# Moving the output weights' means within the filling of a two-layer kernel, with second PSUM banks for projections and center taps

## The chip, the cores and the metric

The kernel runs on one core of a Trainium2 chip. Its engines run side by side, each through its own queue in order, and wait for one another by semaphores: TensorE (PE, the matrix products, which write to PSUM), VectorE (DVE), ScalarE (ACT), GpSimd (POOL, which also issues DMAs that add onto their destination) and SyncE (SP, which only issues DMAs). PSUM has eight banks of 128 partitions by 512 fp32 values. The metric is the time of one execution on the device in microseconds; lower is better.

## The reference, cut to what matters

Two layers work on an image batch of 2 x 768 channels x 64 x 64, all in fp32. Only layer 0 is touched by the change. Cut to its core:

```python
x = gn(x) @ in_proj_w.T                      # 768 -> 1536 channels
xs = depthwise_conv3x3(x, conv_w) + conv_b   # nine taps per channel
xs = xs * sigmoid(xs)                        # SiLU
dt, Bs, Cs = split(xs @ x_proj_w.T, [48, 52])
delta = softplus(dt @ dt_w.T + dt_b)
s[l] = exp(delta * A) * s[l-1] + delta * xs * Bs      # scan over 4096 positions, 4 states
y = sum(s * Cs) + D * xs
y = (y - mean(y)) * rsqrt(var(y) + 1e-5) * ln_g + ln_b
out = x_in + y @ out_proj_w.T
```

Layer 1 (group norm, projection, an attention-like weighting per head, output projection) follows.

The normalization of y is folded into the output weights: a row of the weights (one of the 1536 inner channels) is multiplied by `ln_g`, and from each output column its mean over the 1536 channels is subtracted, so that the mean of y drops out of the product. `ln_b` gives a bias of each output channel. The changed weights are written to DRAM once, and read back from there in layer 0.

## The kernel before

Layer 0 is cut into 16 tiles (eight rows of an image, 512 positions) times 12 chunks of 128 inner channels, 192 units in all. The function `step(g)` issues one step of a software pipeline written out by hand: `manual_schedule` keeps the order of the text on every engine, so the order of the calls in `step` is the order of each queue. One step works on different units at once:

- `n = g + 17`: the projection `in_proj(n)` on TensorE, six chunks of 128 input channels into one bank, then `in_proj_evict(n)`, which ScalarE does into one of two padded buffers `xs_bufs[n % 2]`. For the first 12 units `row0(n)` computes the image's first row apart, into the bank "pz" (`psZ`), and ScalarE copies it to `carry`.
- `a = g + 15`: the nine taps of the 3 x 3 convolution. ScalarE writes the center tap into the PSUM tile `acc` (`tap_act`, issued a step ahead for a + 1), TensorE can add taps onto it with a diagonal (`diag`, `taps_pe`), VectorE adds taps with one fused multiply-add each (`taps_dve`), the last of them writing the result u to SBUF. Some taps go another way: ScalarE multiplies them into buffers (`taps_act`), and GpSimd's DMAs add these up and then onto u (`taps_dma_sum`, `taps_dma`). Tables say which taps go where: `FILL_DMA_TAPS` and `FILL_PE_TAPS` for a < 15.
- `silu(a - 4 ..)` for four units at a time, with a table load of ScalarE ahead and one behind, and then `x_proj_pair` on TensorE; every fourth step.
- `g` itself: softplus, exponentials, the scan on VectorE (`scan`, lines 512 and 514), products with C (line 521), sums by GpSimd and its DMAs.
- `g - 12`: the output projection, with weights read from `wo_dr`.

The first 16 calls, `step(-17)` to `step(-2)`, with v = 0 to 15, are the **filling**: only n and a are in range, so there are projections and taps but no scan. In step v the projection is number v and the taps are those of v - 2. During the filling the statistics of the second image are also gathered (`gn_load`, `gn_piece`, one or two pieces a step on VectorE), and the output weights are made ready in this order:

- in the steps v = 2 to 5, SP loads the 12 chunks of the weights into `wg` (line 246);
- at the end of step 7, `out_weights_rows`: 72 matmuls into a bank "po0", and three copies by ScalarE;
- at the end of step 8, `out_weights_mean`: the sums spread over the partitions into `wm` ("po0", "po1") and the bias into `pb` ("st"), and copies by ScalarE;
- after the steps 8 to 15, one or two chunks each: ScalarE's scaling (line 276) and right behind it the subtraction of the means (line 277), by GpSimd for the first chunk and by VectorE for the second; SP stores a chunk to `wo_dr` after the next step (line 280).

The pool that holds `wg` is closed after the filling, and the buffers of the steady part (B and C in `bc`, `das`, `s`, `tm_bufs`) take its place in SBUF, so they can be written only when the stores have read `wg`. From `step(-1)` on come these buffers, and from `step(0)` the scans.

PSUM in the filling: one bank "psa" for projections (odd ones from n = 12 on also use "po0"), one bank "acc" for center taps, two for "pz", one for "px", "po0", "po1" and "st".

Of the kernel before, what the change touches and what calls it, by code (L numbers as in the profile page):

```python
# [7 lines left out]
F32 = mybir.dt.float32  # L8
# [6 lines left out]
P = 128  # L15
# [6 lines left out]
KM = DM // P  # L22
KI = DI // P
# [21 lines left out]

DMA_TAPS = ((0, 2, 6), (0, 2, 6), (0, 2, 6), (0, 2))
PE_TAPS = ((), (), (), (1, 7))
FILL_DMA_TAPS = ((0, 2), (0, 2), (0, 2), ())  # L50
FILL_PE_TAPS = ((), (), (), (1,))

AHEAD = 15
BEHIND = 12
# [13 lines left out]
def both_layers(  # L68
# [192 lines left out]
            nc.scalar.copy(rows[32 * j : 32 * j + 2, :], gb[32 * j : 32 * j + 2, :MG])  # L261

    def out_weights_mean(rows, wmean, pick):
        pb = psS.tile([P, 512], F32, tag="st", name="pbo")
        wm = [psO.tile([P, 512], F32, tag=f"po{e}", name=f"pwm{e}") for e in range(2)]
        for j in range(KM // 2):
            for e in range(2):
                m = 2 * j + e
                nc.tensor.matmul(pb[:, m : m + 1], rows[:, e * P : (e + 1) * P], pick[:, j, P : P + 1], start=True, stop=True)
            nc.tensor.matmul(wm[j // 2][:, j % 2 * MG : (j % 2 + 1) * MG], pick[:, j, :P], rows, start=True, stop=True)  # L270
        nc.scalar.copy(wmean[:, : 2 * MG], wm[0])
        nc.scalar.copy(wmean[:, 2 * MG :], wm[1][:, :MG])
        nc.scalar.copy(bias_o, pb[:, :KM])

    def out_weights_scale(wg, wmean, k, engine):
        nc.scalar.activation(wg[:, k, :], wg[:, k, :], AF.Copy, scale=pc[:, k, PC_G : PC_G + 1])
        engine.tensor_sub(wg[:, k, :], wg[:, k, :], wmean)

    def out_weights_store(wg, k):
# [63 lines left out]
    def in_proj(n):  # L343
        i, c, b, t = where(n)
        nn = TL if t < NT - 1 or b + 1 < NB else TL - W
        w = wis.pop(n)
        if KI <= n < AHEAD + 2 and n % 2:
            pa = psO.tile([P, 512], F32, tag="po0", name=f"pa{n}")
        else:
            pa = psA.tile([P, 512], F32, tag="psa", name=f"pa{n}")  # L350
        for k in range(KM):
            nc.tensor.matmul(pa[:, :nn], w[:, k, :], xts[i, k][:, :nn], start=(k == 0), stop=(k == KM - 1))  # L352
# [20 lines left out]


    def dma_taps(a):
        return (DMA_TAPS if a >= AHEAD else FILL_DMA_TAPS)[a % 4]

    def pe_taps(a):
        return (PE_TAPS if a >= AHEAD else FILL_PE_TAPS)[a % 4]

    def diag(a):
        c = a % KI
# [3 lines left out]
        dgs[a] = dg  # L386

    def tap_act(a):
        acc = psC.tile([P, 512], F32, tag="acc", name=f"acc{a}")
        nc.scalar.activation(  # L390
            acc.rearrange("p (h w) -> p h w", w=W), xs_bufs[a % 2][:, 1 : 1 + TR, 1 : 1 + W], AF.Copy,
            scale=pc[:, a % KI, PC_W + 4 : PC_W + 5],
        )
        accs[a] = acc
# [47 lines left out]
    def silu(a):  # L442
        nc.scalar.activation(us[a], us[a], AF.Silu, bias=pc[:, a % KI, PC_CB : PC_CB + 1])  # L443
# [667 lines left out]
    with tc.manual_schedule():  # L1111
# [31 lines left out]
        def step(g, prep=None):  # L1143
# [46 lines left out]
            if 0 <= a + 1 < NQ0:  # L1190
                diag(a + 1)

            do_silu = g % 4 == 1 and 0 < a <= NQ0
            do_soft = g % 2 == 1 and 0 <= g + 1 < NQ0
            if do_silu:
                nc.scalar.preload_act_table_set(SILU_SET)
                for q in range(4):
                    silu(a - 4 + q)
            if do_soft:
                nc.scalar.preload_act_table_set(SOFTPLUS_SET)  # L1200
                softplus_pair(g + 1)
# [89 lines left out]
                prep()  # L1291
            if do_silu:
                for q in range(0, 4, 2):
                    x_proj_pair(a - 4 + q)
            if v == len(by_step) + 1:
                gn_aggregate(1)
                norms[g + 2] = gn_finish(1)
# [7 lines left out]
        with tc.tile_pool(name="l0st", bufs=1, side="right") as sp:  # L1305
            wg = sp.tile([P, KI, DM], F32, name="wg")
            rows = sp.tile([P, MG], F32, name="gb_rows")
            nc.vector.memset(rows, 0.0)
            wmean = sp.tile([P, DM], F32, name="wmean")
            pick = sp.tile([P, KM // 2, P + 1], F32, name="pick")  # L1310
            nc.sync.dma_start(pick, pick_in)

            first = -AHEAD - 2
            ready_w = {8: (0,), 9: (1, 2), 10: (3,), 11: (4, 5), 12: (6, 7), 13: (8, 9), 14: (10,), 15: (11,)}
            prep = {7: lambda: out_weights_rows(wg, rows), 8: lambda: out_weights_mean(rows, wmean, pick)}
            for v in range(AHEAD + 1):
# [199 lines left out]
```

## Time and profile before

| | us |
|---|---|
| median of 3 runs | 3758.63 (3756.74 to 3765.8) |
| profiled execution | 3758.2 |
| its span | 3756.3 |

The page adds up each engine's busy time over the span, and then by 40 slices. A digit of 9 is 90% or more of a slice. The filling lies in the first 206 us, some two slices.

| in the filling, from the trace | value |
|---|---|
| projection 1 (line 352, twelve records) starts | 61.96 us |
| taps of unit 0 on VectorE (line 436) start | 70.70 us |
| `out_weights_rows` on TensorE | 113.0 to 118.4 us |
| `out_weights_mean` on TensorE | 125.8 to 128.4 us |
| scaling (line 276), ScalarE | 12, median 927 ns, first 128.9, last 198.4 us |
| subtraction (line 277), GpSimd | 8, 1799 to 2117 ns |
| subtraction (line 277), VectorE | 4, 1853 to 2175 ns |
| stores (line 280), SP | 12, first 131.8, last 201.5 us |
| first scan product (line 512) starts | 209.65 us |

Rows of the order of time have the start in us, the duration in us, engine, line, operation, what is written from what, how many were merged, and in brackets the idle time of the engine just before and what ended it. A row with `u<-xs,pc,acc` is the last tap of a unit. TensorE's merged rows end somewhat late, since ends of matmuls are modelled: the distance from one start to the next is the better measure where rows follow one another closely.

### The profile page before, as it was taken

What the parts mean: (1) busy time and instruction counts of PE and PEld (TensorE: products, weight loads), DVE (VectorE), ACT (ScalarE), POOL (GpSimd) and SP (SyncE); (2) the same over time, 40 slices, a digit from 0 to 9 for tenths busy, and PEclk for the clock granted to TensorE, in tenths of its full rate; (3) what the DMA queues carried; (4) which work ended last, traced back from release to release, by engine and by line L of the source; (5) the groups of instructions that cost most, each with busy time, mean ns of one, the idle gap of its engine ahead of it and who ended that gap; (6) DMA issues with size and microseconds to landing.
All of it is one profiled execution on the core that took longest, in us unless ns stands there. A gap on an engine that the chain in (4) does not pass through costs nothing.

```text
span 3756.3 us, 36987 instructions
## 1 busy us (share of the span) xinstructions
PE 3558.0 (95%) x10882; PEld 1719.9 (46%) x10882; DVE 2842.8 (76%) x2554; ACT 2562.5 (68%) x4940; POOL 1742.7 (46%) x1761
## 2 busy tenths in 40 slices
PE   5877999999999999999999999999999999999999
PEld 3422433333333333333343343333344458886688
DVE  7699999999999999999999999997710162224522
ACT  2588888889888888889788888897633441244221
POOL 0245565555555556555555655654413214320232
PEclk9988999999999999999999999999999999999999
DMA  9677898989989899898898989996656428764487
GB/s 352 182 176 149 187 207 177 209 196 202 203 183 202 190 212 202 186 205 182 200 205 189 211 176 207 201 197 170 150 144 191 141 75 271 253 214 125 150 270 243
DMA packets 371081, 730.80 MB, mean 195 GB/s; under 512 B 43280, under 2 KB 105168, under 8 KB 366784
## 3 DMA queue, kind: packets, MB, share of 16 engines
q0 software_dynamic: 145632, 269.03, 42.1%
q1 hardware_dynamic: 225248, 459.41, 37.2%
q8 instruction: 88, 1.44, 0.2%
q14 instruction: 113, 0.93, 0.1%
HBM read 433.88 MB, written 60.03 MB: 131 GB/s over the span
## 4 chain that ended last, share of the span: by engine, by line
PE 39%; DVE 37%; ACT 10%; DMA 6%; issue 6%; POOL 2%; SPq 0%; DVEq 0%; POOLq 0%; ACTq 0%
DVE s L514 14%; DVE acc L436 8%; PE po_p L852 6%; PE po L574 6%; DVE da L521 6%; DVE s L512 5%; PE pa L352 5%; PE psa_p L852 4%; PE acc_p L852 4%; PE mmp L663 4%; DMA u<-ysum 3%; PE pq L663 3%; PE mmp L694 2%; ACT tm L402 1%; ACT da L489 1%
## 5 line engine op out<-in xcount | busy, mean ns | idle before, releaser
L352 PE MATMUL pa<-u,w 128*128 128x512 f32 (+1 forms) x2304 | 1046.8, 605 | 20.2 <-ACT carry L367 13.6
L574 PE MATMUL po<-u,w 128*128 128x512 f32 x2304 | 1035.9, 599 | 18.5 <-DVE u L586 18.5
L514 DVE TENSOR_TENSOR_SCAN s<-da,s 128x2052 f32<-128x2052 f32 x192 | 851.1, 4433 | 19.5 <-ACT u L307 0.5
L352 PEld LDWEIGHTS pa<-u,w 128*128 128x128 f32 x2304 | 433.8, 193 | 619.4 <-issue 489.6
L574 PEld LDWEIGHTS po<-u,w 128*128 128x128 f32 x2304 | 428.9, 190 | 610.8 <-issue 557.8
L501 POOL TENSOR_TENSOR ysum<-da 128x1024 f32<-128x1024 f32 x192 | 385.0, 2005 | 576.9 <-DVE da L521 467.8
L436 DVE SCALAR_TENSOR_TENSOR acc<-xs,pc,acc 128x512 f32<-128x512 f32 x741 | 558.1, 753 | 39.4 <-PE acc L422 13.0
L489 ACT ACTIVATE da<-dl,neg_a 128x512 f32<-128x512 f32 x768 | 489.7, 713 | 0.0
L512 DVE TENSOR_TENSOR s<-du,bc 128x2048 f32<-128x2048 f32 x192 | 438.8, 2285 | 55.1 <-POOL du L493 54.8
L408 POOL DMA_DIRECT2D tm<-tm x309 | 268.0, 867 | 447.1 <-ACT tm L402 385.1
L521 DVE TENSOR_TENSOR da<-s,bc 128x2048 f32<-128x2048 f32 x192 | 440.0, 2292 | 6.3
L508 POOL DMA_DIRECT2D u<-ysum x384 | 378.8, 1250 | 3.7 <-issue 2.6
L390 ACT ACTIVATE acc<-xs,pc 128x512 f32<-128x512 f32 x192 | 132.3, 689 | 282.5 <-DVE u L436 281.2
L402 ACT ACTIVATE tm<-xs,pc 128x512 f32<-128x512 f32 x486 | 317.1, 717 | 4.8 <-DMA tm<-tm 3.3
L493 POOL TENSOR_TENSOR du<-dl,u 128x512 f32<-128x512 f32 x192 | 244.2, 1272 | 0.0
L414 POOL DMA_DIRECT2D u<-tm x177 | 205.2, 1159 | 56.5 <-issue 29.8
L852 PE MATMUL po_p<-u,w 128*128 128x256 f32 x630 | 159.2, 382 | 0.0
L436 DVE SCALAR_TENSOR_TENSOR u<-xs,pc,acc 128x512 f32<-128x512 f32 x192 | 143.6, 748 | 9.5 <-DVE acc L436 0.4
L477 PE MATMUL pz<-xd,dt_w 48*128 48x512 f32 x384 | 113.6, 670 | 37.0 <-DVE gs_x L193 13.9
L663 PE MATMUL pq<-u,w 128*128 128x512 f32 x312 | 140.4, 596 | 1.9 <-ACT u L651 1.8
L505 ACT ACTIVATE u<-u,pc 128x512 f32<-128x512 f32 x192 | 137.0, 714 | 2.1 <-POOL du L493 2.1
L443 ACT ACTIVATE u<-u,pc 128x512 f32<-128x512 f32 x192 | 124.4, 712 | 15.0 <-DMA u<-tm 14.4
(286 smaller groups left out, 4749.0 us busy)
## 6 DMA issues: line engine op xcount, KB each, us to landing
u<-ysum POOLq DMA_DIRECT2D x384, 256.0 KB, 5.7
tm<-tm POOLq DMA_DIRECT2D x309, 256.0 KB, 4.4
w<-in_wP SPq DMA_DIRECT2D x192, 384.0 KB, 5.1
w<-wo_dr SPq DMA_DIRECT2D x192, 384.0 KB, 4.9
u<-x SPq DMA_DIRECT2D x274, 256.0 KB, 5.4
w<-s_dr_p SPq DMA_DIRECT2D x240, 192.0 KB, 3.7
u<-tm POOLq DMA_DIRECT2D x177, 256.0 KB, 5.8
bc<-bc_dr SPq DMA_DIRECT2D x32, 1024.0 KB, 7.1
```

Of the source, the lines that this page charges most:

```text
L352: nc.tensor.matmul(pa[:, :nn], w[:, k, :], xts[i, k][:, :nn], start=(k == 0), stop=(k == KM - 1))
L402: nc.scalar.activation(tm.rearrange("p (h w) -> p h w", w=W), xs[:, dy : dy + TR, dx : dx + W], AF.Copy, scale=pc[:, c, PC_W + j : PC_W + ...
L436: nc.vector.scalar_tensor_tensor(dst, xs[:, dy : dy + TR, dx : dx + W], pc[:, c, PC_W + j : PC_W + j + 1], acc, ALU.mult, ALU.add)
L489: nc.scalar.activation(das[g % 2][:, n, 1:], deltas[g], AF.Exp, scale=neg_a[:, c, n : n + 1])
L501: nc.gpsimd.tensor_add(ysum[:, 0 : 2 + g % 2 : 1 + g % 2, :], da[:, 0:2, 1:], da[:, 2:4, 1:])
L508: nc.gpsimd.dma_start(us[g], ysums(g, n), accum_op=ALU.add)
L512: nc.vector.tensor_mul(s[:, :, 1:], dus.pop(g).unsqueeze(1).to_broadcast([P, NS, TL]), bc[:, :NS, :])
L514: nc.vector.tensor_tensor_scan(sf, das[g % 2].rearrange("p n l -> p (n l)"), sf, 0.0, ALU.mult, ALU.add)
L521: nc.vector.tensor_mul(das[g % 2][:, :, 1:], s[:, :, 1:], bc[:, NS:, :])
L574: nc.tensor.matmul(po[e], w[:, kk, e * P : (e + 1) * P], us[i * KI + k], start=(k == 0), stop=(k == KI - 1))
L663: nc.tensor.matmul(pa, w[:, k, :], x1s[b, j, k], start=(k == 0), stop=(k == KM - 1))
L852: nc.tensor.matmul(dst, half[:, k, :], tiles[blocks[seq[i][0]][:3]][what][k], start=(start and k == 0), stop=(k == KH - 1), skip_group_che ...
```

## The change

All of it is in the filling.

- The center tap's tile alternates between the banks "st" (even a) and "acc" (odd a) for a < 15. The bias `pb`, which used "st", now lies in the second half of the tile `wm`, and `wm` itself in the two banks of "pz".
- Projections with odd n below 17 use "po1", from n = 1 on; even ones "psa".
- All units of the filling but 11 have the DMA taps 0 and 2 and no PE tap; unit 11 has the PE tap 1 and no DMA taps. Before, this was so for 3, 7 and 11.
- SiLU and `x_proj_pair` of units 0 to 3 move from step 6 to step 8, those of 4 to 7 from step 10 to step 12. Those of 8 to 11 stay in step 14.
- `out_weights_rows` and `out_weights_mean` both move to the end of step 11.
- Chunks are scaled three after each of the steps 11 to 14. Two of three (all three after step 14) are subtracted by GpSimd right behind; the third by VectorE after the following step. All three are stored after the following step.

```diff
-FILL_DMA_TAPS = ((0, 2), (0, 2), (0, 2), ())
-FILL_PE_TAPS = ((), (), (), (1,))
+FILL_DMA_TAPS = (0, 2)
+FILL_PE_TAPS = (1,)
...
     def out_weights_mean(rows, wmean, pick):
-        pb = psS.tile([P, 512], F32, tag="st", name="pbo")
-        wm = [psO.tile([P, 512], F32, tag=f"po{e}", name=f"pwm{e}") for e in range(2)]
+        wm = psZ.tile([P, 2, 512], F32, tag="pz", name="pwm")
+        pb = wm[:, 1, MG : MG + KM]
...
-    def out_weights_scale(wg, wmean, k, engine):
+    def out_weights_scale(wg, k):
         nc.scalar.activation(wg[:, k, :], wg[:, k, :], AF.Copy, scale=pc[:, k, PC_G : PC_G + 1])
+
+    def out_weights_sub(wg, wmean, k, engine):
         engine.tensor_sub(wg[:, k, :], wg[:, k, :], wmean)
...
-        if KI <= n < AHEAD + 2 and n % 2:
-            pa = psO.tile([P, 512], F32, tag="po0", name=f"pa{n}")
+        if n < AHEAD + 2 and n % 2:
+            pa = psO.tile([P, 512], F32, tag="po1", name=f"pa{n}")
...
     def dma_taps(a):
-        return (DMA_TAPS if a >= AHEAD else FILL_DMA_TAPS)[a % 4]
+        return DMA_TAPS[a % 4] if a >= AHEAD else FILL_DMA_TAPS if a != KI - 1 else ()
     def pe_taps(a):
-        return (PE_TAPS if a >= AHEAD else FILL_PE_TAPS)[a % 4]
+        return PE_TAPS[a % 4] if a >= AHEAD else FILL_PE_TAPS if a == KI - 1 else ()
+    def silu_of(a):
+        if a < KI:
+            return {6: 0, 10: 4}.get(a)
+        return a - 4 if a % 4 == 0 and a <= NQ0 else None
...
     def tap_act(a):
-        acc = psC.tile([P, 512], F32, tag="acc", name=f"acc{a}")
+        bank, tag = (psS, "st") if a < AHEAD and a % 2 == 0 else (psC, "acc")
+        acc = bank.tile([P, 512], F32, tag=tag, name=f"acc{a}")
...
-            do_silu = g % 4 == 1 and 0 < a <= NQ0
+            first4 = silu_of(a)
+            do_silu = first4 is not None
...
-                    silu(a - 4 + q)
+                    silu(first4 + q)
...
-                    x_proj_pair(a - 4 + q)
+                    x_proj_pair(first4 + q)
...
-            ready_w = {8: (0,), 9: (1, 2), 10: (3,), 11: (4, 5), 12: (6, 7), 13: (8, 9), 14: (10,), 15: (11,)}
-            prep = {7: lambda: out_weights_rows(wg, rows), 8: lambda: out_weights_mean(rows, wmean, pick)}
+            scaled_w = {11: ((0, 1), (2,)), 12: ((3, 4), (5,)), 13: ((6, 7), (8,)), 14: ((9, 10, 11), ())}
+            def means():
+                out_weights_rows(wg, rows)
+                out_weights_mean(rows, wmean, pick)
             for v in range(AHEAD + 1):
                 if 2 <= v < 6:
                     out_weights_load(wg, 3 * (v - 2))
-                step(first + v, prep.get(v))
+                step(first + v, means if v == 11 else None)
...
-                for k, engine in zip(ready_w.get(v, ()), (nc.gpsimd, nc.vector)):
-                    out_weights_scale(wg, wmean, k, engine)
-                for k in ready_w.get(v - 1, ()):
+                now, late_w = scaled_w.get(v, ((), ()))
+                for k in now + late_w:
+                    out_weights_scale(wg, k)
+                for k in now:
+                    out_weights_sub(wg, wmean, k, nc.gpsimd)
+                now, late_w = scaled_w.get(v - 1, ((), ()))
+                for k in late_w:
+                    out_weights_sub(wg, wmean, k, nc.vector)
+                for k in now + late_w:
                     out_weights_store(wg, k)
-            for k in ready_w[AHEAD]:
-                out_weights_store(wg, k)
```

More of the change, by code (lines that the diff above doesn't have):

```diff
@@ L269, in out_weights_mean @@
                 nc.tensor.matmul(pb[:, m : m + 1], rows[:, e * P : (e + 1) * P], pick[:, j, P : P + 1], start=True, stop=True)
[L270 to L273, printed above, removed]
-    def out_weights_scale(wg, wmean, k, engine):
+            nc.tensor.matmul(wm[:, j // 2, j % 2 * MG : (j % 2 + 1) * MG], pick[:, j, :P], rows, start=True, stop=True)
+        nc.scalar.copy(wmean[:, : 2 * MG], wm[:, 0, :])
+        nc.scalar.copy(wmean[:, 2 * MG :], wm[:, 1, :MG])
+        nc.scalar.copy(bias_o, pb)
+    def out_weights_scale(wg, k):
         nc.scalar.activation(wg[:, k, :], wg[:, k, :], AF.Copy, scale=pc[:, k, PC_G : PC_G + 1])
+    def out_weights_sub(wg, wmean, k, engine):
         engine.tensor_sub(wg[:, k, :], wg[:, k, :], wmean)
```

## The prediction

> **What bounds it now.** I read the page first, then the busy time by stage, the waits of the filling, and its order of time engine by engine. Starts are us from the span's start; the second number is the duration.
>
> ```profile
> span 3756.3 us, 36987 instructions
> PE 3558.0 (95%) x10882; PEld 1719.9 (46%) x10882; DVE 2842.8 (76%) x2554; ACT 2562.5 (68%) x4940; POOL 1742.7 (46%) x1761
> DVE  7699999999999999999999999997710162224522
> PEclk9988999999999999999999999999999999999999
> ```
>
> The 40 slices are 94 us each. From slice 3 to 27 VectorE is at 9 tenths: there every step waits for it, at about 12.9 us a step (the first scan products start at 209.65, 223.90, 236.81, 249.71). In front of that lies the filling, the only place where the change acts. So I ask one thing: when does the steady part start? In the trace its first taps start at 206.61 and the first scan product at 209.65. From 206.6 to 260 VectorE has under 0.4 us of idle time, so an earlier start isn't soaked up.
>
> ```profile
> ACT acc L390 <- DVE u L436: 37.8, 13, 7.4
> DVE wg L277 <- ACT wg L276: 20.8, 4, 7.9
> DVE acc L436 <- PE acc L422: 13.0, 2, 8.8
> PE acc L422 <- ACT acc L390: 7.1, 1, 7.1
> ```
>
> These are the waits from 60 to 210 us (total, times, longest). The first is the single bank of the center taps: ScalarE can't write the next one before VectorE is through with the last. The second is VectorE's share of the mean subtraction. The third is the PE tap of channels 3 and 7. They form one ring:
>
> ```profile
> 160.87 2.13 DVE L277 TENSOR_TENSOR wg<-wg,wmean 128x768 f32<-128x768 f32 x1 [7.91 <-ACT wg L276]
> 162.92 3.91 DVE L436 SCALAR_TENSOR_TENSOR acc<-xs,pc,acc 128x512 f32<-128x512 f32 x5
> ...
> 167.71 0.69 ACT L390 ACTIVATE acc<-xs,pc 128x512 f32<-128x512 f32 x1 [6.59 <-DVE u L436]
> ...
> 168.46 2.07 PE L422 MATMUL acc<-xs,dg 128*128 128x512 f32 x2 [7.14 <-ACT acc L390]
> 170.32 11.84 PE L352 MATMUL pa<-u,w 128*128 128x512 f32 x24
> ```
>
> VectorE's subtraction waits for a scaling that ScalarE queues behind the eviction of the next projection; the taps, whose data lie ready, stand behind it; ScalarE waits for the taps, TensorE for ScalarE.
>
> ```profile
> 73.66 1.45 PE L338 MATMUL pa<-u,w 128*128 128x64 f32 x12
> 77.09 7.11 PE L352 MATMUL pa<-u,w 128*128 128x512 f32 x12 [1.99 <-ACT carry L367]
> 84.04 1.45 PE L338 MATMUL pa<-u,w 128*128 128x64 f32 x12
> 85.33 5.37 PE L352 MATMUL pa<-u,w 128*128 128x512 f32 x12
> 75.00:85.00 10.00, 8.01 (x23) 3.93 (x22) 9.43 (x14) 4.55 (x12) 1.72 (x2) 0.83 1.06 352
> ```
>
> Up to projection 11 TensorE is nearly without gaps, except where a projection waits for the single bank (n = 3 and n = 11). The last line is the stage from 75 to 85: granted clock 0.83, and that projection took 7.11 instead of 5.2.
>
> **The change, part by part.** I run the filling again by rows. Pitches (start to start): projection 5.21 (61.96 to 67.17), its row of halo 1.28, six VectorE taps 4.6, a statistics piece 0.6, center tap 0.63, eviction 0.85, two DMA-tap products 1.24, halo copy 0.2, four SiLUs with two table loads 5.15, one scaling 0.83. Step v holds projection v and the taps of a = v - 2.
>
> *Second bank for projections, from n = 1.* Projection 3 no longer waits for eviction 2, since eviction 1 was over at 68.1; it starts at 74.94 behind its halo row and ends at 80.15, not 84.2. Then TensorE takes 6.49 a step: projections 4 to 8 end at 86.6, 93.1, 99.6, 106.1, 112.6. ScalarE has under 4 us of work in each such step and VectorE 5.2 to 5.9, so TensorE sets the pace. Weights come two steps ahead and no wait for them is in the trace; DMA is full until 110, but each load keeps over 5 us of margin.
>
> *Second bank for center taps; DMA taps for a = 3 and 7.* This removes two pairs of PE matmuls (0.86 each), two diagonals (0.4) and two VectorE taps (0.77), and adds four ScalarE products (0.62 each) and four GpSimd DMA issues (0.86), on engines that are two thirds idle there. The 4.21 and 8.78 us that VectorE sat before taps 3 and 7 go. What is late next is TensorE.
>
> *SiLU of 0 to 3 and 4 to 7 two steps later.* Its 5.15 us are the same. In step 8 it hides behind projections 8 and 9 (VectorE waits 4.9 us, TensorE doesn't); the four pairs behind it cost TensorE 1.87. So projections 9, 10, 11 end at 121.0, 127.5, 134.0. Before, projection 11 ended at 155.1: 21 us ahead, of which 7.9 are the means' matmuls, not yet done.
>
> *The means behind projection 11 (the twelfth).* Rows 5.3 (72 matmuls), ScalarE's copies of them 1.1, which TensorE now waits for as both parts stand in one step, means 2.6: TensorE is free at 143.2 for projection 12, which ends at 148.4 (before, about 161.3; 13 us ahead). ScalarE copies the means by 143.5, scales three weights until 146.0, makes a diagonal, then the SiLUs of 4 to 7, and writes center tap 11 only at 152.3. TensorE waits 4 us for it, VectorE, done with taps 10 at 137, some 15. This is the new wait; behind it stand eviction 12 and everything else.
>
> *From there*, at the rates that the trace shows after an idle TensorE: PE tap 2.0, four pairs 2.9, projection 13 5.9, so it ends at 163.2. Taps 11 on VectorE (seven) run 154.4 to 159.8. Eviction 13, taps and three scalings end at 167.9, the SiLUs of 8 to 11 at 173.0, their pairs at 172.9, projection 15 at 178.3; the sum of halves and the copy at 180.6 (before 196.4). To the steady part's first taps it was 10.2 us; without the scaling of weight 11 in between it is 9.4: **190.0 instead of 206.6, so 16.6 us**. VectorE and GpSimd hide behind this: taps 12, 13, 14 start at 163.1, 173.8, 179.7 (before 184.9, 190.4, 196.2).
>
> *Subtractions.* VectorE has three of 12 instead of four, and each comes a step after its scaling, so the 20.8 us of waits go nearly whole. GpSimd has nine. Its last three run from 176.7 at 2.1 each to 183.0 (before, the last ended at 201.5); in front of them wait the DMA taps of 13. The stores of all twelve are on SP, each at the end of the next step, and SP's later weight loads stand behind them: the load for projection 16 is issued at about 163.5 and used at 182. The last store must land before the broadcast of B and C: 183.4 plus 2.6, plus 5 to land, is 191, before the scan product at 193.1. Cover: 2 us.
>
> [...] The trace gave projection 3 a clock of 0.83 and 7.11 us after only 1.99 us of idleness, projection 11 the same 7.11 after 1.95. [...] The rows make the removed gaps worth 3.85 each and the new ones about 4 together: 16.6. [...]
> [...] The rows: 2.09 us on GpSimd, 1.85 to 2.17 on VectorE while both ran, and by the scan product's rate (2.284 us for 2048) about 0.86 alone. On VectorE twelve would cost 10 us in the taps' queue; on GpSimd two a step with two DMA issues are 5.9 us in steps of 8 and more, off the path. [...]
>
> **Rivals.**
> 1. *Forecast, 0.58:* 16.6 us less, 3741.6 for a span of 3756.3; the profiled run took 3758.2, 0.4 under the median of 3758.63. I say 3742. Own range 3736 to 3747: full rate throughout gives 20.6 us (3738), some handoffs of 0.1 to 0.2 less.
> 2. *The lead is partly given back before the first scan, 0.22:* ScalarE stays the bound from 143 on, or GpSimd's last three drag the stores. For a gain under 11 us, the scan product would start after 198.6, and a subtraction take (198.6 - 176.7 - 8.1) / 3 = 4.6 us. For: all of it hangs on one ScalarE queue and 2 us of cover. Against: eight rows between 1.80 and 2.12. Time: 3750.
> 3. *Slower, 0.10:* the steady steps lengthen. VectorE idles there for about 103 us in 185 steps, 0.56 a step, 32.2 of it on GpSimd's product of delta and u, which queues behind DMA issues that wait for landings. The changed takings permute the slots' order, and transfers meet otherwise. From 0.09 us more a step (16.6 / 185) the lead is gone; at 0.18 it is 3775. Against: queue orders and the number of free slots are unchanged there, and VectorE paces it.
> 4. *The second banks don't help, 0.10:* the two xs buffers hold evictions to the taps anyway, and what remains is the subtraction's waits less the new stall: about 5 us, 3753. Against: eviction n needs only taps n - 2, which my chain has ready.
>
> **Chances.** 0.3% is 11.3 us, about what a measurement of this kernel can tell. Faster by more: case 1 nearly whole, some of 2: 0.66. Within: most of 2, case 4 and some of 3: 0.23. Slower: 0.11. Range 3734 to 3755.
>
> **What would show it.** Right: the first scan product near 193; the ScalarE wait for u before center taps nearly gone; no wait before projection 3; a gap of some 4 us on TensorE between projection 12 and the PE taps of 11; nine GpSimd rows near 2.1 us. Wrong: subtractions over 4 us, projections late for weights, or VectorE's idle time in the steady part up by 10 us.

## The result, and the profile after

| | before | after |
|---|---|---|
| median of 20 runs each | 3763.36 us (3756.74 to 3767.24) | 3753.17 us (3745.89 to 3760.16) |
| profiled execution, its span | 3758.2, 3756.3 | 3754.5, 3752.5 |
| first taps of the steady part | 206.61 | 191.35 |
| first scan product | 209.65 | 196.83 |
| from the first scan's product to the last's | 2518.6 | 2525.9 |
| from the last scan's product to the end | 1028.1 | 1029.7 |

The ratio is 0.9974 [0.9967, 0.9981]: 10.2 us less, where 16.6 were forecast. The three runs shown before the change had a median 4.7 us below that of the 20, so a gain has to be taken from runs made side by side. The lower rows, from one profiled execution of each, show where to look: the first scan product starts 12.8 us sooner, and what follows takes 7.3 us more up to the last scan. A second profile of each kernel (below) has 15.5 us of the first and 3.0 of the second.

The page of the kernel after, its span, busy totals, and the 40 slices of VectorE and of the granted clock:

```profile
span 3752.5 us, 36993 instructions
PE 3553.2 (95%) x10878; PEld 1717.3 (46%) x10878; DVE 2841.8 (76%) x2551; ACT 2564.3 (68%) x4942; POOL 1747.9 (47%) x1766
DVE  8699999999999999999999999997710162224522
PEclk9988999999999999999999999999999999999999
```

On this scale hardly anything moves (the first digit of VectorE is 8 instead of 7): the difference is a tenth of one slice. The waits from 60 to 210 us of the kernel after (total, times, longest), first VectorE's, then ScalarE's:

```profile
DVE wg L280 <- ACT wg L277: 11.9, 2, 11.0
DVE acc L446 <- ACT acc L400: 7.5, 2, 4.7
DVE acc L446 <- PE acc L432: 7.4, 1, 7.4
...
ACT xs L367 <- DVE acc L446: 6.3, 5, 3.7
ACT xs L368 <- DVE u L446: 6.1, 3, 2.0
...
ACT acc L400 <- DVE u L446: 0.8, 1, 0.8
```

ScalarE's 37.8 us before center taps are gone but for 0.8; 12.4 us of its waits for VectorE stand before evictions and their copies (`xs`) instead. The first row is no longer a loss in every unit: 11.0 of it is one wait, VectorE idle behind taps 10 until the means are there and the first weights scaled. TensorE in order of time, and the stages from 75 to 85 and from 150 to 160 us (the column before the last two is the granted clock), kernel after:

```profile
74.52 5.37 PE L355 MATMUL pa<-u,w 128*128 128x512 f32 x12
79.72 1.45 PE L341 MATMUL pa<-u,w 128*128 128x64 f32 x12
...
143.70 6.41 PE L355 MATMUL pa<-u,w 128*128 128x512 f32 x12
153.61 2.05 PE L432 MATMUL acc<-xs,dg 128*128 128x512 f32 x2 [3.50 <-issue]
155.58 3.68 PE L460 MATMUL px<-u,xp_w 128*64 128x512 f32 x8
...
75.00:85.00 10.00, 10.00 (x34) 5.21 (x33) 9.71 (x14) 5.95 (x14) 1.72 (x2) 1.00 1.06 351
150.00:160.00 10.00, 6.50 (x13) 1.84 (x13) 4.13 (x6) 7.70 (x13) 6.97 (x5) 0.66 0.93 243
```

Projection 3 follows its halo row without a wait, at clock 1.00. The new gap stands where the prediction put it, between projection 12 and the PE tap of unit 11, and from 150 to 160 us the clock is 0.66. Projection 12 itself took 6.41 us instead of 5.2: it stands behind the means, with 1.22 us of waiting and 3 us of small products ahead of it, and the clock from 144 to 146 us was 0.52.

The end of the filling, VectorE in order of time, kernel after:

```profile
191.35 2.34 DVE L446 SCALAR_TENSOR_TENSOR acc<-xs,pc,acc 128x512 f32<-128x512 f32 x3 [5.06 <-ACT tm L412]
193.72 0.75 DVE L446 SCALAR_TENSOR_TENSOR u<-xs,pc,acc 128x512 f32<-128x512 f32 x1
196.83 2.29 DVE L522 TENSOR_TENSOR s<-du,bc 128x2048 f32<-128x2048 f32 x1 [2.36 <-DMA bc<-bc_dr]
```

Before, the scan product stood right behind the last tap (208.98, then 209.65). Now it waits 2.36 us, by the record for the broadcast of B and C. The chain of waits of the kernel after (start, duration, what) and GpSimd's order of time show what is behind it:

```profile
180.82 2.96 POOL wg L280 x2
183.79 3.55 DMA wo_dr<-wg
187.34 0.02 SPq L480
187.36 0.05 issue
187.41 9.04 DMA bc<-bc_dr
```

```profile
192.29 0.86 POOL L424 DMA_DIRECT2D u<-u  x1 [4.53 <-DVE acc L446]
192.83 1.21 POOL L418 DMA_DIRECT2D tm<-tm  x1
193.39 1.94 POOL L503 TENSOR_TENSOR du<-dl,u 128x512 f32<-128x512 f32 x1
```

The last subtraction, the stores behind it and then 9.04 us for the broadcast to land: 196.45. Had it landed in the forecast's 5, the product of delta and u (`du`, ended at 195.33) would still have held the scan product back to about 195.4, for some 0.9 us of the 2.36.

### The profile page after: what moved, and what is told of

It reads as the page before. It is cut to its first block, busy times and chain, and to the rows that moved or that the text cites. A ratio compares the mean times of both kernels' runs of the same rounds, so it can differ in the third digit from the quotient of the medians.

```text
span 3752.5 us, 36993 instructions
## 1 busy us (share of the span) xinstructions
PE 3553.2 (95%) x10878; PEld 1717.3 (46%) x10878; DVE 2841.8 (76%) x2551; ACT 2564.3 (68%) x4942; POOL 1747.9 (47%) x1766
## 4 chain that ended last, share of the span: by engine, by line
DVE 39%; PE 35%; ACT 7%; issue 7%; DMA 6%; POOL 3%; DVEq 0%; SPq 0%; POOLq 0%; ACTq 0%
DVE s L524 15%; DVE acc L446 8%; DVE s L522 6%; DVE da L531 6%; PE po_p L862 6%; PE po L584 5%; PE psa_p L862 4%; PE acc_p L862 4%; PE mmp L673 4%; DMA u<-ysum 3%; PE pq L673 3%; PE pa L355 3%; PE mmp L704 2%; ACT tm L412 1%; POOL ysum L511 1%
## 5 line engine op out<-in xcount | busy, mean ns | idle before, releaser
L522 DVE TENSOR_TENSOR s<-du,bc 128x2048 f32<-128x2048 f32 x192 | 438.9, 2286 | 62.7 <-POOL du L503 60.3
L424 POOL DMA_DIRECT2D u<-tm x177 | 205.1, 1159 | 54.8 <-issue 37.1
L368 ACT COPY xs<-pa 128x512 f32<-128x512 f32 (+1 forms) x192 | 109.7, 571 | 45.0 <-PE pa L355 38.9
L515 ACT ACTIVATE u<-u,pc 128x512 f32<-128x512 f32 x192 | 137.1, 714 | 2.8 <-POOL du L503 2.7
```

What stands on the lines that cost most here:

```text
L522: nc.vector.tensor_mul(s[:, :, 1:], dus.pop(g).unsqueeze(1).to_broadcast([P, NS, TL]), bc[:, :NS, :])
```

## The experiments

Each edit is against the kernel after, if nothing else is said. A kernel's own run of "before" is the one on the same chip at the same time. In the tables "product" is the start of the first scan product, "stretch" the time from the first scan to the last, both from the profiled run, "us" the median. Single draws of the stretch differ by some 2 us in one kernel (before 2518.6 and 2520.4; after 2525.9 and 2523.4) and by more between kernels that should be alike, so one draw of it says little.

**Which part shortened the filling?** Both kernels again, unedited, give the second draw; then parts are done or undone one by one.

> The kernel before once more, for a second draw of its profile. Theory A (the lead is lost to scatter: the first profile of the kernel before was a fast draw): first scan product at 209.7 within 1 us, and 2521 to 2526 us from the first to the last scan instead of 2518.6. Theory B (the change makes the steady part longer): again 2518 to 2520.

> The changed kernel once more, for a second draw of its steady part. Theory A (the filling's lead of 12.8 us at the first scan passes to the end, and the rest is scatter of the steady part): first scan product again at 196.8 within 0.5, time 8 to 13 us below the kernel before. Theory B (the steady part itself has become longer): the stretch from the first to the last scan is again about 7 us longer than the 2518.6 of the kernel before, and the gain is under 8 us.

`before_subs_later` is the kernel before with one part of the change: VectorE subtracts a step after the scaling.

```diff
-                for k, engine in zip(ready_w.get(v, ()), (nc.gpsimd, nc.vector)):
-                    out_weights_scale(wg, wmean, k, engine)
+                for k in ready_w.get(v, ()):
+                    out_weights_scale(wg, k)
+                for k in ready_w.get(v, ())[:1]:
+                    out_weights_sub(wg, wmean, k, nc.gpsimd)
+                for k in ready_w.get(v - 1, ())[1:]:
+                    out_weights_sub(wg, wmean, k, nc.vector)
```

> The kernel before with one edit: VectorE's four subtractions come a step after their scalings, as in the changed kernel; means, banks and taps stay. Theory A (the ring through the subtraction is what held the filling): first scan product 8 to 10 us earlier, near 200. Rival (the single banks and the PE taps hold it, and the wait only moves): under 3 us, 207 or later.

`one_proj_bank` takes the second bank of the projections away before n = 12, `one_tap_bank` that of the center taps, `no_second_banks` both:

```diff
-        if n < AHEAD + 2 and n % 2:
+        if KI <= n < AHEAD + 2 and n % 2:
...
-        bank, tag = (psS, "st") if a < AHEAD and a % 2 == 0 else (psC, "acc")
+        bank, tag = (psC, "acc")
```

> The changed kernel with one bank for projections below 12, as before. Theory A (the bank removes one wait, before projection 3, and the slow projection behind it; elsewhere the halo row covers the eviction): projection 3 waits 2 us and takes 7.1 instead of 5.2, and the first scan product comes 3.9 us later, at 200.7. [...] Rival 4 of the prediction (the bank does nothing): 196.8.

> The changed kernel with one bank for center taps, as before. Theory A (TensorE at 6.5 us a step sets the pace and VectorE has slack): the waits of ScalarE for VectorE's last tap come back, 25 us and more in total, but the first scan product moves by under 1 us. Rival (the 37.8 us of such waits in the kernel before lay on the path): it comes 5 us later or more, at 202.

> The changed kernel with neither second bank: one for projections below 12 and one for center taps. Theory A (each bank alone removes the wait before projection 3, so one is spare): 2 to 4 us later than the changed kernel at the first scan product, 198 to 200. Rival (neither is needed once the subtractions have left): within 1 us of it.

`pe_taps_3_7` gives units 3 and 7 their PE tap back, instead of the DMA taps:

```diff
-        return DMA_TAPS[a % 4] if a >= AHEAD else FILL_DMA_TAPS if a != KI - 1 else ()
+        return DMA_TAPS[a % 4] if a >= AHEAD else FILL_DMA_TAPS if a % 4 != 3 else ()
...
-        return PE_TAPS[a % 4] if a >= AHEAD else FILL_PE_TAPS if a == KI - 1 else ()
+        return PE_TAPS[a % 4] if a >= AHEAD else FILL_PE_TAPS if a % 4 == 3 else ()
```

> The changed kernel with PE taps for units 3 and 7 again and no DMA taps for them: GpSimd issues four DMAs fewer in the filling, and two buffers fewer are taken from the list of slots for each of the two units. Theory A (the order of slots or of the DMAs' semaphores, set in the filling, lengthens the steady part): first to last scan 2518 to 2521 us as in the kernel before, steps 119 and 120 at 13.2 and 14 to 16 us instead of 15.0 and 16.9. Theory B (the longer steady part comes from elsewhere, the earlier start for one): 2522 to 2527, steps 119 and 120 as in the changed kernel. First scan product 1 to 2 us later than 196.8 in either.

| kernel | us | before | ratio | product | stretch |
|---|---|---|---|---|---|
| before_again | 3764.35 | 3763.11 | 1.0003 [0.9994, 1.0011] | 211.49 | 2520.4 |
| after_again | 3752.03 | 3761.88 | 0.9971 [0.9960, 0.9983] | 196.01 | 2523.4 |
| before_subs_later | 3748.11 | 3763.11 | 0.9962 [0.9948, 0.9976] | 197.41 | 2518.2 |
| one_proj_bank | 3754.59 | 3761.88 | 0.9979 [0.9969, 0.9988] | 195.39 | 2526.8 |
| one_tap_bank | 3752.96 | 3761.88 | 0.9973 [0.9963, 0.9984] | 195.16 | 2521.3 |
| no_second_banks | 3753.41 | 3763.11 | 0.9979 [0.9972, 0.9987] | 197.01 | 2525.1 |
| pe_taps_3_7 | 3752.55 | 3762.88 | 0.9971 [0.9958, 0.9984] | 199.84 | 2518.6 |

The later subtraction alone brings the first scan product to 197.41, within 1.4 us of the whole change (196.83, 196.01). VectorE in order of time, kernel before_subs_later:

```profile
159.81 2.14 DVE L279 TENSOR_TENSOR wg<-wg,wmean 128x768 f32<-128x768 f32 x1 [1.01 <-ACT wg L276]
161.87 4.71 DVE L438 SCALAR_TENSOR_TENSOR acc<-xs,pc,acc 128x512 f32<-128x512 f32 x6
...
168.47 0.94 DVE L279 TENSOR_TENSOR wg<-wg,wmean 128x768 f32<-128x768 f32 x1
...
174.55 0.94 DVE L279 TENSOR_TENSOR wg<-wg,wmean 128x768 f32<-128x768 f32 x1
```

Where VectorE sat 7.91 us before one subtraction, it now waits 1.01 or not at all; the waits of this kind fall from 20.8 to 2.6 us. Two of the four subtractions also take 0.94 us instead of 1.85 to 2.17. In the kernel after, the one at 162.30 takes 0.94 us as well, with no subtraction of GpSimd's beside it. That breaks the ring of the prediction at one place, and the ring's other members don't matter any more. The banks show it from the other side: without either, or without both, the product starts between 195.16 and 197.01, and the taps of unit 15 ahead of it between 191.03 and 192.71 (191.35 and 192.00 in the two draws of the kernel after). In `one_tap_bank` ScalarE's wait for VectorE is back (26.7 us in ten waits) and costs nothing. In `no_second_banks` projection 3 waits again, TensorE in order of time:

```profile
76.86 5.42 PE L355 MATMUL pa<-u,w 128*128 128x512 f32 x12 [1.43 <-ACT carry L370]
```

It takes 5.42 us, not 7.11, and the clock stays at 1.00 from 75 to 85 us. The DMA taps of units 3 and 7 are worth some 3 us of filling (199.84), and yet `pe_taps_3_7` isn't slower, since its stretch is that of the kernel before. That was the first hint to the loss.

**What does the new gap cost?** `warm_gap` adds four matmuls behind projection 12, whose results nobody reads (each fp32 matmul has two records, so the four stand as x8); they fill the gap with work, but let nothing start sooner.

```diff
+            if a + 1 == KI - 1:
+                warm = psO.tile([P, 512], F32, tag="po0", name="warm")
+                for _ in range(4):
+                    nc.tensor.matmul(warm, ident, wg_held[0][:, KI - 1, :512], start=True, stop=True)
             if 0 <= a + 1 < NQ0:
                 taps_pe(a + 1)
```

> The changed kernel with four idle 128x512 products on TensorE in its gap between projection 12 and the PE tap of unit 11; nothing reads them. Theory A (the idle gap slows what comes behind it): the PE tap takes 0.9 instead of 2.05 and the four pairs 1.9 instead of 3.7, projection 13 ends 3 us earlier, and the first scan product comes at 194 or a little later. Rival (they are slow for another reason, or ScalarE alone sets what follows): no more than 0.5 us earlier.

`no_pe_tap_11` leaves that tap to VectorE, `silu_later` puts the SiLUs of units 4 to 7 a step later, away from the copies of the means and the scalings behind them, and `subs_done_early` ends the scalings a step sooner (four a step, two for each engine):

```diff
-        return PE_TAPS[a % 4] if a >= AHEAD else FILL_PE_TAPS if a == KI - 1 else ()
+        return PE_TAPS[a % 4] if a >= AHEAD else ()
```

> The changed kernel with all eight outer taps of unit 11 on VectorE. Theory A (TensorE stands still behind the PE tap of unit 11, and projection 13 and all that follows with it): projection 13 ends about 3 to 5 us earlier, and the first scan product comes 2 to 4 us earlier, near 193.5. Rival (ScalarE's queue holds it, not TensorE's): under 1 us.

```diff
-            return {6: 0, 10: 4}.get(a)
+            return {6: 0, 11: 4}.get(a)
```

> The changed kernel with SiLU and products of units 4 to 7 in step 13 instead of 12. Theory A (center tap 11 waits behind the means, the scalings and the SiLUs on ScalarE): the gap of TensorE before the PE tap of unit 11 goes from 4 to 5 us to under 1, and the first scan product comes 3 to 6 us earlier, near 192. Rival (ScalarE has the same work in sum and is the bound from 143 us on): under 1 us.

```diff
-            scaled_w = {11: ((0, 1), (2,)), 12: ((3, 4), (5,)), 13: ((6, 7), (8,)), 14: ((9, 10, 11), ())}
+            scaled_w = {11: ((0, 1), (2, 3)), 12: ((4, 5), (6, 7)), 13: ((8, 9), (10, 11))}
```

> The changed kernel with four weights scaled after each of the steps 11 to 13, two subtracted by GpSimd and two by VectorE a step later, and all stored by the end of step 14. Theory A (the first scan product is held by several things within a few us: the broadcast, then GpSimd's product of delta and u): the wait for the broadcast goes, the first scan product comes 0 to 1.5 us earlier. Rival (the broadcast alone holds it): 2.4 us earlier, at 194.4.

| kernel | us | before | ratio | product | stretch |
|---|---|---|---|---|---|
| warm_gap | 3750.05 | 3761.88 | 0.9965 [0.9953, 0.9978] | 194.07 | 2524.2 |
| no_pe_tap_11 | 3750.12 | 3762.88 | 0.9966 [0.9954, 0.9978] | 191.95 | 2525.7 |
| silu_later | 3749.32 | 3762.88 | 0.9964 [0.9952, 0.9976] | 188.65 | 2523.2 |
| subs_done_early | 3755.79 | 3763.11 | 0.9980 [0.9972, 0.9988] | 196.87 | 2522.8 |

TensorE in order of time, kernel warm_gap, and then kernel silu_later:

```profile
151.25 3.60 PE L1303 MATMUL warm<-wg,ident 128*128 128x512 f32 x8
154.68 1.02 PE L432 MATMUL acc<-xs,dg 128*128 128x512 f32 x2
155.63 1.94 PE L460 MATMUL px<-u,xp_w 128*64 128x512 f32 x8
```

```profile
143.06 5.31 PE L355 MATMUL pa<-u,w 128*128 128x512 f32 x12
148.21 1.02 PE L432 MATMUL acc<-xs,dg 128*128 128x512 f32 x2
149.07 5.31 PE L355 MATMUL pa<-u,w 128*128 128x512 f32 x12
```

Kept busy, TensorE takes 1.02 us for the PE tap instead of 2.05, and 1.94 for the pairs instead of 3.68: 2.8 us, and the clock from 150 to 160 us is 1.00 instead of 0.66. The product comes 2 to 3 us sooner, although projection 1 had started 1.3 us later in this run. With the SiLUs a step later there is no gap at all: the PE tap starts at 148.21 instead of 153.61, and the product comes 8.2 us sooner, of which up to 1.1 are due to projection 12 (5.31 us instead of 6.41, with the clock at 1.00). So the new gap is due to five microseconds of SiLUs and table loads (1.28, 2.56 and 1.28) right behind the means' copies and the first three scalings on ScalarE. `no_pe_tap_11` shows it from TensorE's side: with nothing there to wait for ScalarE, projection 13 starts at 152.54 instead of 159.19, and the product comes 4 to 5 us sooner. The medians tell less of `silu_later` (13.6 us under before, against 10.2 of the kernel after); its interval reaches 4.5 us to either side, that of the kernel after 2.6. `subs_done_early` shows that the stores were not alone in holding the first scan back: its product waits for no broadcast, but its taps of 15 start 2.5 us later (193.83), and it gains nothing.

**Where does the steady part lose?** By means, the nine profiles with four DMAs of GpSimd more than before have a stretch of 2524.3 us (2521.3 to 2526.8), the four with as many as before 2519.0 (2518.2 to 2520.4). The distance from one scan's start to the next scatters by up to 1.7 us in single steps, without an order that I could find; at three places these two groups are far apart. (At three others, after scans 49, 59 and 129, they are 0.4 to 0.7 us apart by means, the other way.) Numbering scans from 0, the distances after scans 78, 119 and 120:

| kernel | GpSimd DMAs in the filling, against before | after 78 | after 119 | after 120 |
|---|---|---|---|---|
| before; before_again | 0 | 12.96; 12.96 | 13.16; 13.16 | 14.12; 15.95 |
| before_subs_later | 0 | 12.96 | 13.16 | 14.12 |
| pe_taps_3_7 | 0 | 13.03 | 13.16 | 14.13 |
| after; after_again | +4 | 13.75; 13.75 | 15.05; 14.85 | 16.99; 16.98 |
| the other seven above | +4 | 13.75 to 13.76 | 14.63 to 15.20 | 15.82 to 17.20 |

The kernel after loses 5.6 us in these three steps (45.8 against 40.2), about what its stretch is longer by. It isn't the earlier start: `before_subs_later` starts as early and loses nothing. What the kernels that lose have in common are the four DMAs of GpSimd that the DMA taps of units 3 and 7 add. My first theory was a turn: if these DMAs take eight semaphores in rotation, four more change which of them share one, and which wait for which. Four more, which GpSimd issues in the steps 2 to 5 into a tile that nobody reads, would bring the old turn back, with all else (the buffers' order too) as in the kernel after:

```diff
+            extra = sp.tile([P, 4], F32, name="extra")
...
+                    nc.gpsimd.dma_start(extra[:, v - 2 : v - 1], pick_in[:, 0, :1])
```

> The changed kernel with four small DMAs more on GpSimd in the steps 2 to 5 (4 bytes of each partition, read by nobody): eight more than in the kernel before, so that the eight semaphores that the DMAs take in turn meet the same DMAs as there; the slots stay in the changed kernel's order. If the semaphores' turn lengthens the steady part: steps 119 and 120 at 13.2 and 14 to 16. If it is the slots' order, or neither: 15.0 and 16.9 as in the changed kernel.

`eight_more_dmas` issues two in each of these steps, so it has the turn of the kernel after. `silu_later_turn` joins the four DMAs to the later SiLUs:

```diff
+                    for e in range(2):
+                        nc.gpsimd.dma_start(extra[:, 2 * (v - 2) + e : 2 * (v - 2) + e + 1], pick_in[:, 0, :1])
```

> The changed kernel with eight small DMAs more on GpSimd in the steps 2 to 5 (read by nobody): twelve more than in the kernel before, so the eight semaphores stand as in the changed kernel. Theory A (their turn lengthens steps 119 and 120): 15.0 and 16.9 us again. [...]

> The changed kernel with the SiLUs of units 4 to 7 in step 13 and four small DMAs more (read by nobody). Both effects add up: first scan product at 188.7 within 1 us as with the SiLUs alone, 2519 to 2522 us from the first to the last scan, and 18 to 21 us below the kernel before. Rival (a gain in the filling is lost in the steady part, whatever the turn): 12 to 15 us below.

| kernel | us | before | ratio | product | stretch | after 78, 119, 120 |
|---|---|---|---|---|---|---|
| four_more_dmas (+8) | 3748.67 | 3762.88 | 0.9969 [0.9957, 0.9980] | 195.50 | 2521.6 | 12.96, 13.16, 14.12 |
| eight_more_dmas (+12) | 3750.91 | 3762.48 | 0.9967 [0.9955, 0.9979] | 195.02 | 2523.6 | 13.22, 13.16, 14.12 |
| silu_later_turn (+8) | 3743.76 | 3762.48 | 0.9950 [0.9937, 0.9962] | 190.96 | 2518.8 | 12.96, 13.16, 14.12 |

Four more restore the steps, but so do eight more: the theory of the turn falls. The traces bear this out: GpSimd's DMAs take eight semaphores in turn (111 to 118, in all 1038 and 1042 DMAs of the kernels before and after), and the sum that stands late in the step after scan 119 of the kernel after has the same one in `eight_more_dmas`, where it isn't late. What is left is that with exactly four DMAs more than before these three steps are longer, and with none, eight or twelve more they are not; why, I can't say. Nor is it shown that twelve more cost nothing: the stretch of `eight_more_dmas` is as long as that of after_again, and its step after scan 97 took 14.59 us, where every other run has 12.89. So that a larger number of DMAs ahead lengthens other steps instead isn't ruled out. And `silu_later_turn` missed its forecast of 188.7 for the product by 2.3 us: projection 12 took 6.59 us again. What happens in such a step can be read. VectorE in order of time, kernel after, and then GpSimd:

```profile
1784.49 2.29 DVE L522 TENSOR_TENSOR s<-du,bc 128x2048 f32<-128x2048 f32 x1 [1.81 <-POOL du L503]
...
1793.90 0.17 DVE L641 TENSOR_SCALAR mv<-mv 128x12 f32<-128x12 f32 x1
1794.11 2.00 DVE L643 TENSOR_TENSOR msq<-mv,stats 128x6 f32<-128x6 f32 x1
1796.15 1.20 DVE L644 TENSOR_TENSOR msq<-msq 128x6 f32<-128x6 f32 x1
```

```profile
1770.37 0.88 POOL L418 DMA_DIRECT2D tm<-tm  x1 [1.42 <-ACT acc L400]
...
1781.23 2.00 POOL L511 TENSOR_TENSOR ysum<-da 128x1024 f32<-128x1024 f32 x1 [5.83 <-DVE acc L446]
...
1794.09 2.00 POOL L511 TENSOR_TENSOR ysum<-da 128x1024 f32<-128x1024 f32 x1 [3.43 <-DVE mv L641]
1796.06 1.26 POOL L503 TENSOR_TENSOR du<-dl,u 128x512 f32<-128x512 f32 x1
```

And the same place in the kernel four_more_dmas, VectorE and then GpSimd:

```profile
1791.27 0.17 DVE L643 TENSOR_TENSOR msq<-mv,stats 128x6 f32<-128x6 f32 x1
1791.47 0.17 DVE L644 TENSOR_TENSOR msq<-msq 128x6 f32<-128x6 f32 x1
```

```profile
1767.96 0.85 POOL L418 DMA_DIRECT2D tm<-tm  x1
...
1792.17 2.00 POOL L511 TENSOR_TENSOR ysum<-da 128x1024 f32<-128x1024 f32 x1 [4.60 <-DVE mv L646]
```

After scan 119 the scan product waits 1.81 us for `du`. It is late because GpSimd's sum of the tap buffers had stood 1.42 us a step ahead, and the sums of y behind it landed late (the chain of waits has 9.57 us for them). The record puts these 1.42 us down to a center tap of ScalarE, and in all nine profiles with the longer step the sum starts 0.01 to 0.21 us behind that tap; but in `four_more_dmas` the same sum starts without a wait, and ahead of the tap. No landing of a GpSimd DMA ends the wait either (the nearest, at 1769.44, is 0.93 us ahead). What the sum waited for stays open, and so does the step after scan 78.

After scan 120, two products of 128 by 6 values take 2.00 and 1.20 us instead of 0.17 each, 2.86 more in all, which is the step's whole loss. They end when GpSimd's `ysum` (1796.09) and `du` (1797.32) end. In `four_more_dmas` `ysum` is held until 0.9 us after the first of them has begun, and VectorE is through with both. How little decides here is seen in `before_again`, the one kernel without added DMAs that took longer in this step (15.95); its VectorE and then its GpSimd in order of time:

```profile
1804.43 0.17 DVE L635 TENSOR_TENSOR mv<-mv,msq 128x6 f32<-128x6 f32 x1
1804.63 2.00 DVE L636 TENSOR_SCALAR mv<-mv 128x6 f32<-128x6 f32 x1
```

```profile
1804.61 2.00 POOL L501 TENSOR_TENSOR ysum<-da 128x1024 f32<-128x1024 f32 x1 [4.28 <-DVE mv L635]
```

`ysum` came 0.02 us before the last of the small instructions, and that one stood for 2.00 us.

**Do earlier means pay as well?** `means_early_silu_later` puts the rows back to the end of step 6 and the means to step 7 (into the banks "po0" and "px"), scales two weights in each of the steps 7 to 12, and keeps the later SiLUs and the four DMAs:

```diff
-        wm = psZ.tile([P, 2, 512], F32, tag="pz", name="pwm")
+        wm = [psO.tile([P, 512], F32, tag="po0", name="pwm0"), psX.tile([P, 512], F32, tag="px", name="pwm1")]
...
-            scaled_w = {11: ((0, 1), (2,)), 12: ((3, 4), (5,)), 13: ((6, 7), (8,)), 14: ((9, 10, 11), ())}
+            scaled_w = {7 + j: ((2 * j,), (2 * j + 1,)) for j in range(6)}
...
+            prep = {6: lambda: out_weights_rows(wg, rows), 7: lambda: out_weights_mean(rows, wmean, pick)}
...
-                step(first + v, means if v == 11 else None)
+                step(first + v, prep.get(v))
```

> As silu_later_turn, with the rows of the means at the end of step 6 and the means at the end of step 7 (in the banks po0 and px), and two weights scaled after each of the steps 7 to 12, one subtracted by GpSimd and one by VectorE a step later. Theory A (from projection 11 on ScalarE's queue is the bound, and the means stood in its way): first scan product 3 to 5 us earlier than with silu_later, 184 to 186, and 22 to 26 us below the kernel before. Rival (TensorE pays for the means in any place, and two subtractions a step hold up GpSimd's taps): no earlier than 188.

It takes 3744.89 us, 0.9950 [0.9936, 0.9964], no better than `silu_later_turn` at 3743.76. Its taps of 15 start at 184.22, seven microseconds sooner than in the kernel after, but its first scan product at 191.20, after 3.85 us of idleness in wait for a DMA, so here the landings ahead of the first scan hold it back. Whether earlier means would pay without that wait isn't shown.

## Why the prediction was right in the filling and wrong in the sum

**Right.** No wait before projection 3; TensorE sets the pace of the filling up to the means (projection 11 ended at 133.8, forecast 134.0); ScalarE's waits for u gone; the new gap where it was said (3.5 and 4.0 us in the two draws; forecast 4); nine GpSimd subtractions, seven of 1.8 to 2.1 us and the first two of 2.5. The steady part's first taps were forecast at 190.0 and started at 191.35 and 192.00. The rows were a good guide to the slow matmuls: with their waits gone, projections 3 and 11 took 5.37 us instead of 7.11, and the new gaps, put at about 4 together, cost 2.8 behind the gap before the PE tap of unit 11 (`warm_gap`) and up to 1.1 in projection 12. No run shows the 20.6 us of full rate throughout, on which the low end of the range rests; with the clock at 1.00 from 150 to 160 us (`warm_gap`) the first scan product came 16.5 us ahead of the mean of the two draws before.

**Wrong, first: "an earlier start isn't soaked up".** This step failed, and by the two draws it accounts for most of the miss. I had checked 50 us behind the first scan, where VectorE has no idle time, and the lead did hold there. It was lost far away, for the most part at three single steps: the mean stretch of the two draws is 2524.7 against 2519.5, so 5.2 us, and the three steps alone are 4.5 us longer by the same means. The slower rival had the place right (steady steps lengthen), with a size of 0.03 us a step rather than 0.09 (5.2 / 191), but in three steps and not in all; and its cause is not the one: the order of the buffers is the same in `four_more_dmas`, which doesn't lose in these steps. VectorE's waits for `du` grew less than that (54.8 and 54.9 to 60.3 and 56.6 us from 250 to 2740); the rest sits in instructions that look busy.

**Wrong, second: the terms "2.6, plus 5 to land" and "Cover: 2 us".** The last subtraction ended at 183.8 (forecast 183.0), the last store had landed 3.55 later, and the broadcast took 9.04: 196.45, not 191. In the second draw `du` was last, 0.90 us behind. `du` was no term of my sum at all; it stands behind the DMA tap of unit 14, which waited 4.53 us. Together with taps 1.4 and 2.0 us late, the first scan product came 3.7 and 2.9 us after the forecast's 193.1.

**Right for a wrong reason: the filling's gain by parts.** My chain took 3.85 us for each of two gaps that the second bank of the projections removes, and the ring's waits from the banks, the DMA taps and the later subtraction together. The runs show that the later subtraction alone yields as much as all of it (`before_subs_later`), and the banks nothing that can be told from zero; that a sum of wrong parts came within 2 us at the taps of unit 15 is in part luck. (The change without the later subtraction was not run, so its other parts may break the ring as well.) The fourth rival said so of the banks, but then expected about 5 us of the subtraction's waits less the new stall; alone they were worth 13. My 3.85 had taken the wait before projection 3 for a fixed one. It depends on when the taps of unit 0 start, and these wait for a load (VectorE 2.55 us, up to 69.42, in the kernel before): in the two draws of the kernel before it was 1.99 and 2.51 us, in `before_subs_later`, the same kernel up to there, 1.10, with the clock at 1.00 from 75 to 85 us. The wait before projection 11 went with the ring (1.95 us before, 0.32 in `before_subs_later`).

**The sum.** By means of two draws the filling gave 14.2 us (210.57 to 196.42 at the scan product), the steady part took 5.2, the tail changed by nothing that stands out of its scatter: 9 us, and the medians say 10.2. The change as a whole was not what gained them: it contains one edit that brings about 15 us alone, one (the SiLUs right behind the means) that costs 4.5 to 8 in the filling (195.50 to 190.96 from `four_more_dmas` to `silu_later_turn`, 196.83 to 188.65 from after to `silu_later`), and one (the DMA taps of units 3 and 7) that gains 3 there and loses at least as much later. With these two put right it is `silu_later_turn`, 18.7 us under the kernel before; by the intervals of both that is not surely more than `before_subs_later` gains with its one edit.

## What to carry to other kernels

When waits form a ring, ask which single one breaks it, and try that alone before counting the others' removal as gains. An instruction that waits for another engine is best issued where its operand is long done: here one step later, at no cost, was worth as much as the whole change. A lead won at the start must be followed to the end, scan by scan: compare distances between equal events of both kernels, and look at the steps that differ, durations of short instructions included.

## What the runs showed of the hardware that I had not expected

- VectorE's instructions that ran long beside one of GpSimd's ended at its end or shortly behind it: the two small products took 2.00 and 1.20 us instead of 0.17, ending within 0.03 us of `ysum` and `du`. The subtraction of 128 by 768 takes 0.94 us alone (at 162.30 in the kernel after). In the profiles of the kernels before and after, the five of VectorE's subtractions that began while GpSimd ran one took 1.85 to 3.10 us, and each ended 0.82 or 0.83 us behind GpSimd's last one beside it. In the prediction I had read "1.85 to 2.17 on VectorE while both ran" as a rate of the subtraction. Not everything ran long: beside GpSimd's subtractions of 155.30 six taps, with one of their two tensors in PSUM, took the same 4.71 us as elsewhere. VectorE and then GpSimd in order of time, kernel after:

```profile
155.69 4.71 DVE L446 SCALAR_TENSOR_TENSOR acc<-xs,pc,acc 128x512 f32<-128x512 f32 x6 [7.36 <-PE acc L432]
...
169.29 3.10 DVE L280 TENSOR_TENSOR wg<-wg,wmean 128x768 f32<-128x768 f32 x1 [0.83 <-ACT wg L277]
```

```profile
155.30 3.58 POOL L280 TENSOR_TENSOR wg<-wg,wmean 128x768 f32<-128x768 f32 x2 [1.90 <-ACT wg L277]
...
167.70 3.87 POOL L280 TENSOR_TENSOR wg<-wg,wmean 128x768 f32<-128x768 f32 x2
```

- TensorE was slow behind some short waits and not behind others. Before projection 3, waits of 1.99 us (`before`, clock 0.83 from 75 to 85 us) and 2.51 us (`before_again`) were followed by 7.11 us for it, waits of 0.65 (`one_proj_bank`), 1.10 (`before_subs_later`) and 1.43 us (`no_second_banks`) by 5.42. Projection 12 stood behind only 1.22 us of waiting and then 3 us of small products, and took 6.41 us in the kernel after (clock 0.52 from 144 to 146 us), 5.31 in `silu_later` (clock 1.00). Nothing was varied here to find what decides.
- With four DMAs of GpSimd more in the filling, three steps more than 1000 us later were longer in all nine profiles of such kernels: 13.75 to 13.76, 14.63 to 15.20 and 15.82 to 17.20 us after scans 78, 119 and 120, against 12.96, 13.16 and 14.12 in the kernel before. With eight more they took 12.96, 13.16 and 14.12, with twelve 13.22, 13.16 and 14.12. What carries this is open.
